# Reordering one step of a windowed-attention and mixture-of-experts kernel: key products ahead of the norm transposes, and norms one row earlier

## The chip, the cores and the metric

The kernel runs on one core of one Trainium2 chip. The metric is the device time of one execution in microseconds (us); lower is better.

## The reference, cut to what matters

The input `x` is 2 images of 128 channels and 256 by 256 pixels, in fp32. Two blocks follow each other, each with its own residual.

```python
x = x + conv(ln_over_channels(x))          # windowed attention
t = tokens(x)                              # one token per pixel, 128 wide
t = t + ffn(ln_over_channels(t))           # 8 experts, the best 2 of them
```

In the attention, `qkv` is a 1x1 product with a 384x128 weight. Queries are 8x8 pixel windows, keys and values are the 12x12 windows around them, in 4 heads of 32. Relative position logits and a fixed mask are added before the softmax. The mask keeps only keys whose row and column distance to the query are of one parity, so the picture falls apart into four independent planes (even or odd rows, even or odd columns). `W_out` is a last 128x128 product. In the feed-forward block a router gives 8 logits per token; the two highest are kept as gates; each token is the gated sum of two experts' 128x128 products.

## The kernel before, in words

A strip is 8 image rows; there are 64 strips (32 for each image). Each strip has four planes, and the main loop makes one step for each plane: `n` counts planes, `i, pl = divmod(n, 4)` gives the strip and the plane in it. In step `n` three things run interleaved:

- **Attention of plane n.** `scores` makes the logits: 16 small products with `au` (L357) and 64 of 64x32 with keys and queries (L372), which run on quarters of the array, then one exponential on ScalarE into `pT`. `attend` makes the sums (`ones`, L391) and 64 small products with the values (L399), then on VectorE `sT`, `rc`, `rT` and the scaled result `o`. `out_project` is the product `po` (L424), which VectorE adds to `xt`.
- **Projections of plane n+1** (`project`, a generator). Before the change its first part makes `pq` (queries) and `pu` (for the position logits), which VectorE brings into `au` by two transposes and two copies (L290 to L300); its second part has POOL gather `xcol` (L305) and makes the two `pk` products (keys, L312), copied by ScalarE to `kcol`; its third part makes `pvv` (values, L329) from `xcol`.
- **Norms, router and experts of finished rows.** `norms` transposes two rows of the strip before (`px_f`) and two rows of a strip ahead (`px_c`) on TensorE (L211), takes their variance on VectorE (`bn_stats`, L213), and gets the reciprocal root through ScalarE. `ln1_c` spreads the result over partitions by four transposes `pb` (L262) and multiplies into `xn` (L265), the normalised input of `project`. `route` turns the logits (`plt`, L444, and `plg`, L466) into `gate` and `gx` in a chain of small VectorE operations (L470 to L496). `experts`, also a generator, runs one step later than its `route`: `pg` transposes the gate (L505) and ScalarE copies it, `pbias` (L511) starts the sum, then four parts of two 128x512 products `pe` each (L520), of which VectorE adds four experts (L531) and ScalarE scales the other four (L535) and POOL adds those (L536 to L540). Another step later `py` (L544) transposes the sum back.

TensorE executes its instructions in program order. The order inside a step is written by hand as a sequence of calls, with `next(...)` between them pulling the generators on; the framework's scheduler keeps that order per engine nearly everywhere and inserts semaphore waits. `parts` is the newest `experts` generator, `behind` the one before it (its `py`), `ahead` is `project`.

All products outside the attention scores share four PSUM buffers (`mm_tile`, `bufs=4`), handed out in turn, so a product can wait for a reader of an earlier one. `xn`, `xcol`, `kcol` and `auT` each have two buffers. A strip's `xn` needs the last two of its rows copied to the next strip's `xn` by POOL (`halo`, L246).

On TensorE the order of a steady step is: pg, L357, L372, px_f, px_c, plt, pbias, pe (t=0), py, ones L391, L399, pe (t=1), plg, pb, pe (t=2), po, pq, pu, pe (t=3), pk, pk, pvv.

Of the kernel before, what the change touches and what calls it, by code (L numbers as in the profile page):

```python
# [10 lines left out]
F32 = mybir.dt.float32  # L11
# [5 lines left out]
P = 128  # L17
# [21 lines left out]
NU = 9  # L39
# [3 lines left out]
def kernel(  # L43
# [16 lines left out]
    nc = tc.nc  # L60
    B, C, H, W = x.shape
    NS = H // R
    PR, PC = R // 2, W // 2
    NP = PC // 8
# [10 lines left out]
    work = ctx.enter_context(tc.tile_pool(name="work", bufs=2))  # L75
# [4 lines left out]
    def mm_tile(name):  # L80
        return ps_mm.tile([P, 512], F32, tag="mm", name=name)
# [8 lines left out]
    strips = [(b, s) for b in range(B) for s in range(NS)]  # L90
# [89 lines left out]
    wrel = ctile([P, P], "wrel")  # L180
# [4 lines left out]
    auT = []  # L185
# [48 lines left out]
    def ln_rows(i):  # L234

        s = strips[i][1]
        return range(1 if s == 0 else 2, KR - 1 if s == NS - 1 else KR)

    def halo(i):

        s = strips[i][1]
        cur = xn[i % 2]
        if s == 0:
            nc.gpsimd.memset(cur[:, :, :, 0, :], 0.0)
        else:
# [12 lines left out]
    def ln1_c(i, k, rs):  # L258

        pb = mm_tile(f"pb{i}_{k}")  # L260
        for t in range(NT):
            nc.tensor.transpose(  # L262
                pb[:, t * P : (t + 1) * P], rs[:, t : t + 1].broadcast_to([P, P]), ident
            )
        nc.vector.tensor_tensor(  # L265
            xn[i % 2][:, :, :, k, 1 : PC + 1],
            ln1_src(i, k).rearrange("p (y j x) -> p y x j", y=2, x=2),
            pb.rearrange("p (y j x) -> p y x j", y=2, x=2),
            ALU.mult,
        )  # L270

    def project(n, state):

        i, pl = divmod(n, 4)
        xp = xn[i % 2][:, pl // 2, pl % 2]
        inner = xp[:, 1 : 1 + PR, 1 : PC + 1]

        pq = mm_tile(f"pq{n}")
        nc.tensor.matmul(pq, lhsT=wq, rhs=inner, start=True, stop=True)  # L279
        qs = work.tile([P, 2 * NP, PR, 4], F32, tag="qs", name=f"qs{n}")  # L280
        nc.scalar.copy(
            qs.rearrange("p m a s -> p a m s"), pq.rearrange("p (a m s) -> p a m s", a=PR, s=4)
        )

        pu = mm_tile(f"pu{n}")
        nc.tensor.matmul(pu, lhsT=wrel, rhs=inner, start=True, stop=True)  # L288
        uT = work.tile([P, PR, 4, 32], F32, tag="uT", name=f"uT{n}")
        nc.vector.transpose(uT, pu.rearrange("p (a m s) -> p a s m", a=PR, s=4))  # L290
        for j in range(2):
            shifted = uT[:, :, :, NU * j + 3 : NU * j + 9]
            dims = [list(d) for d in shifted.ap]
            dims[1 + j][0] -= 1
            nc.vector.tensor_copy(
                auT[n % 2][:, :, :, 6 * j : 6 * j + 6],
                bass.AP(shifted.tensor, shifted.offset, dims),
            )
        au = work.tile([P, 2 * NP, PR, 4], F32, tag="au", name=f"au{n}")
        nc.vector.transpose(au.rearrange("p m a s -> p a s m"), auT[n % 2])  # L300
        yield

        xl, kk = xcol[n % 2], kcol[n % 2]
        for half in range(2):
            nc.gpsimd.tensor_copy(  # L305
                xl[:, :, half, 0:NK].rearrange("p t (r c) -> p t r c", c=KC),
                windows(xp, half * HP, HP),
            )
        for r in range(0, KR, 3):
            pk = mm_tile(f"pk{n}_{r}")  # L310
            nk = 3 * (PC + 2)
            nc.tensor.matmul(  # L312
                pk[:, :nk],
                lhsT=wk,
                rhs=xp[:, r : r + 3, :].rearrange("p r c -> p (r c)"),
                start=True,
                stop=True,
            )
            nc.scalar.copy(
                kk[:, :, r * KC : (r + 3) * KC].rearrange("p t (r c) -> p t r c", c=KC),  # L320
                windows(pk[:, :nk].rearrange("p (r c) -> p r c", r=3), 0, NP),
            )
        yield

        vv = work.tile([P, HP, P], F32, tag="vv", name=f"vv{n}")
        for t0 in range(0, HP, 4):
            pv = mm_tile(f"pvv{n}_{t0}")
            for t in range(4):
                nc.tensor.matmul(  # L329
                    pv[:, t * P : (t + 1) * P],  # L330
                    lhsT=xl[:, t0 + t].rearrange("p a k -> p (a k)"),
                    rhs=wv,
                    start=True,
                    stop=True,
                )
            nc.scalar.copy(vv[:, t0 : t0 + 4, :].rearrange("p t c -> p (t c)"), pv)  # L336
        state.update(qs=qs, kk=kk, au=au, vv=vv)
        yield
# [82 lines left out]
    def out_project(n, state):  # L421
        i, pl = divmod(n, 4)
        po = mm_tile(f"po{n}")
        nc.tensor.matmul(  # L424
            po, lhsT=wo, rhs=state["o"].rearrange("p f z -> p (f z)"), start=True, stop=True
        )
        xv = xt[i].rearrange("p (a y) (m s x) -> p y x m a s", y=2, x=2, s=4)[:, pl // 2, pl % 2]
        nc.vector.tensor_add(xv, po.rearrange("p (m a s) -> p m a s", a=PR, s=4), xv)

    def norms(f, c, nm):  # L430


        st = small.tile([P, 2 * NT, 6], F32, tag="st", name=f"st{nm}", bufs=4)
        n0, n1 = (0 if f else NT), (2 * NT if c else NT)
        lT = None
        if f:
            src = rows_of(*f)
            stats(src, st, f"f{nm}")
        if c:
            stats(ln1_src(*c), st[:, NT:, :], f"c{nm}")  # L440
        if f:
            plt = mm_tile(f"plt{nm}")
            for t in range(NT):
                nc.tensor.matmul(  # L444
                    plt[32 * t : 32 * t + 32, :P],
                    lhsT=rw,
                    rhs=src[:, t * P : (t + 1) * P],
                    start=True,
                    stop=True,
                )  # L450
            lT = work.tile([P, P], F32, tag="lT", name=f"lT{nm}")
            nc.scalar.copy(lT, plt[:, :P])  # L452
        if not (f or c):
            return None, None, None
        r = rstd(st[:, n0:], epsc[:, n0:n1], n1 - n0, nm)
        return (r[:, 0:NT] if f else None), (r[:, NT - n0 :] if c else None), lT
# [96 lines left out]

    halo(0)
    for k in ln_rows(0):
        ln1_c(0, k, norms(None, (0, k), f"_{k}")[1])
    n_planes = 4 * len(strips)
    states = {0: {}}  # L560
    for _ in project(0, states[0]):
        pass
# [1 line left out]
    parts, behind = none, none  # L564
    for n in range(n_planes + 6):
        i, pl = divmod(n, 4)
        live = n < n_planes
        if pl == 0:
            load_x(i + 3)
            if i + 1 < len(strips):  # L570
                halo(i + 1)
        next(parts, None)
        if live:
            scores(n, states[n])
        f = (i - 1, pl) if 0 < i <= len(strips) else None
        rows = list(ln_rows(i + 1))[-4:] if i + 1 < len(strips) else []
        ks = [k for k in rows if (k - 2) % 4 == pl or (k == 1 and pl == 0)]
        if i + 1 < len(strips) and strips[i + 1][1] == 0:
            ks = list(ln_rows(i + 1))[pl::4]
        rf, rc, lT = norms(f, (i + 1, ks[0]) if ks else None, f"_{n}")  # L580
        next(parts, None)
        next(parts, None)
        next(behind, None)
        if live:
            attend(n, states[n])
        next(parts, None)
        routed = (*f, *route(*f, rf, lT)) if f else None
        if ks:
            ln1_c(i + 1, ks[0], rc)
            for k in ks[1:]:  # L590
                ln1_c(i + 1, k, norms(None, (i + 1, k), f"_{n}_{k}")[1])
        next(parts, None)
        if live:
            out_project(n, states.pop(n))
        ahead = none
        if n + 1 < n_planes:
            states[n + 1] = {}
            ahead = project(n + 1, states[n + 1])
        next(ahead, None)
        next(parts, None)  # L600
        next(ahead, None)
        next(ahead, None)
        behind = parts
        parts = experts(*routed) if routed else none


def shape_constants():
# [55 lines left out]
```

## Time and profile before

| | |
|---|---|
| median of 3 runs | 5855.48 us (5855.04 to 5867.62) |
| profiled execution | 5851.49 us; its span 5849.7 us, 1.8 us lie around it |
| TensorE (PE) busy, matmuls | 5470.1 us, 94% of the span |
| VectorE (DVE) / ScalarE (ACT) / POOL busy | 4262.2 / 2504.6 / 2057.8 us |
| mean granted TensorE clock | 0.974 |
| instruction fetch, TensorE's queue (q8) | 755 packets, 12.37 MB |

How to read it: matmul busy time is no measure of distance from the limit, because matmuls overlap; where a step's length is wanted, the start of one L357 group is compared with the start of the next. Times of a step are given below from the start of its L357 group. DVE instructions overlap by about 0.1 us, so a chain is summed from start to start. "issue" is time in which an engine waited for nothing that the profile shows.

### The profile page before, as it was taken

How to read it: one execution, taken by the hardware profiler on the slowest of the kernel's cores; microseconds unless marked ns; L12 is line 12 of the kernel's file. 1: busy time of each engine (PE TensorE's matmuls, PEld its weight loads, DVE VectorE, ACT ScalarE, POOL GpSimd, SP SyncE). 2: the span in 40 equal slices, each digit the busy share in tenths (PEclk: the TensorE clock that was granted, in tenths of full speed). 3: DMA queues.
4: the chain of work that ended last, by engine and by line, in shares of the span. 5: the costliest groups of instructions: out<-in, count | busy, mean ns of one | idle time of the engine just before them, and what ended most of it. 6: DMA issues, size and time to landing. Idle time of an engine off the chain costs nothing.

```text
span 5849.7 us, 221084 instructions
## 1 busy us (share of the span) xinstructions
PE 5470.1 (94%) x95758; PEld 3226.5 (55%) x95758; DVE 4262.2 (73%) x14184; ACT 2504.6 (43%) x7189; POOL 2057.8 (35%) x3667
## 2 busy tenths in 40 slices
PE   6999999999999999999999999999999999999998
PEld 4555555555555555555555555555555555555554
DVE  4767777767767777767767777767767767767766
ACT  2434444444444444444444444444444434434444
POOL 1333333333333333333333333333333333333334
PEclk8999999999999999999999999999999999999998
DMA  1000000000000000000000000000000000000000
GB/s 51 17 31 17 31 24 23 31 17 31 31 17 31 31 17 31 31 17 31 17 31 31 17 31 28 20 31 17 31 31 17 31 24 24 31 17 31 17 9 23
DMA packets 21957, 149.32 MB, mean 26 GB/s; under 512 B 2906, under 2 KB 4602, under 8 KB 4602
## 3 DMA queue, kind: packets, MB, share of 16 engines
q1 hardware_dynamic: 18432, 134.23, 6.1%
q8 instruction: 755, 12.37, 0.9%
q14 instruction: 216, 1.77, 0.1%
q10 hardware_dynamic: 2554, 0.95, 0.1%
HBM read 68.06 MB, written 67.11 MB: 23 GB/s over the span
## 4 chain that ended last, share of the span: by engine, by line
PE 83%; DVE 8%; ACT 6%; issue 2%; DMA 0%; ACTq 0%; POOL 0%; POOLq 0%; DVEq 0%
PE pe L520 32%; PE pvv L329 7%; PE att L372 6%; ACT others L535 6%; PE att L399 5%; PE pbias L511 5%; PE pk L312 4%; PE pq L279 3%; PE pu L288 3%; PE po L424 3%; PE att L357 3%; PE px_f L211 3%; PE att L391 3%; PE py L544 2%; PE px_c L211 2%
## 5 line engine op out<-in xcount | busy, mean ns | idle before, releaser
L520 PE MATMUL pe<-ew,xt 128*128 128x512 f32 x4096 | 2071.4, 629 | 184.0 <-ACT others L535 184.0
L535 ACT ACTIVATE others<-pe,gx 128x128 f32<-128x128 f32 x4096 | 1199.5, 369 | 1874.0 <-PE pe L520 1869.3
L536 POOL TENSOR_TENSOR others<-others 128x256 f32<-128x256 f32 x1024 | 758.3, 741 | 3324.8 <-ACT others L535 3226.3
L531 DVE SCALAR_TENSOR_TENSOR acc<-pe,gx,acc 128x128 f32<-128x128 f32 x4096 | 1394.6, 340 | 339.6 <-PE pe L520 301.3
L520 PEld LDWEIGHTS pe<-ew,xt 128*128 128x128 f32 x4096 | 725.8, 193 | 1123.1 <-issue 542.0
L213 DVE BATCH_NORM_STATS2 st<-px_f 128x6 f32<-128x128 f32 x1024 | 228.3, 286 | 959.8 <-PE px_f L211 959.8
L539 POOL TENSOR_TENSOR acc<-acc,others 128x128 f32<-128x128 f32 x1024 | 479.0, 468 | 262.8 <-DVE acc L531 207.1
L329 PEld LDWEIGHTS pvv<-wt,xcol 128*128 128x128 f32 x4096 | 476.9, 191 | 154.3 <-ACT others L535 114.6
L329 PE MATMUL pvv<-wt,xcol 128*128 128x128 f32 x4096 | 522.8, 281 | 1.7
L540 POOL TENSOR_TENSOR acc<-acc,others 128x128 f32<-128x128 f32 x1024 | 468.1, 457 | 75.6
L372 PE MATMUL att<-qs,kcol 32*64 32x32 f32 x32768 | 404.7, 225 | 68.5 <-issue 68.2
L380 ACT ACTIVATE pT<-att 128x1024 f32<-128x1024 f32 x256 | 262.3, 1025 | 445.1 <-PE att L372 445.1
L372 PEld LDWEIGHTS att<-qs,kcol 32*64 32x64 f32 x32768 | 396.0, 130 | 74.1 <-issue 73.5
L312 PE MATMUL pk<-xn,wt 128*128 128x390 f32 x1024 | 378.0, 491 | 0.0
L399 PEld LDWEIGHTS att<-pT,vv 64*32 64x32 f32 x32768 | 351.6, 105 | 47.5 <-issue 9.9
L336 ACT COPY vv<-pvv 128x512 f32<-128x512 f32 x512 | 300.8, 587 | 165.5 <-PE pvv L329 165.5
L399 PE MATMUL att<-pT,vv 64*32 64x32 f32 x32768 | 348.8, 201 | 5.5 <-issue 5.0
L305 POOL COPY xcol<-xn 128x480 f32<-128x480 f32 x512 | 302.1, 613 | 120.5 <-DVE xn L265 76.4
L511 PE MATMUL pbias<-eb,gT 32*128 32x512 f32 x512 | 311.7, 690 | 2.8 <-ACT lT L452 2.1
L312 PEld LDWEIGHTS pk<-xn,wt 128*128 128x128 f32 x1024 | 195.6, 191 | 194.9 <-issue 91.6
L424 PE MATMUL po<-o,wt 128*128 128x512 f32 x512 | 264.9, 599 | 12.8 <-DVE o L418 12.8
L300 DVE STREAM_TRANSPOSE au<-auT 128x512 f32<-128x512 f32 x256 | 270.5, 1057 | 0.2
(3777 smaller groups left out, 7019.7 us busy)
## 6 DMA issues: line engine op xcount, KB each, us to landing
xt<-in_x_dram SPq DMA_DIRECT2D x64, 1024.0 KB, 4.8
out_dram<-xt SPq DMA_DIRECT2D x64, 1024.0 KB, 5.2
ew<-in_L_ffn_expert_w_dram ACTq DMA_DIRECT2D x1, 512.0 KB
wall<-in_L_conv_W_qkv_dram ACTq DMA_DIRECT2D x1, 192.0 KB
keys<-in_c_keys_dram ACTq DMA_DIRECT2D x1, 64.0 KB, 7.5
wall<-in_L_conv_W_out_dram ACTq DMA_DIRECT2D x1, 64.0 KB
eb<-in_L_ffn_expert_b_dram ACTq DMA_DIRECT2D x4, 4.0 KB
ties<-in_c_ties_dram ACTq DMA_DIRECT2D x1, 32.0 KB
```

Source lines behind the costliest of these rows:

```text
L312: nc.tensor.matmul(pk[:, :nk], lhsT=wk, rhs=xp[:, r : r + 3, :].rearrange("p r c -> p (r c)"), start=True, stop=True,)
L329: nc.tensor.matmul(pv[:, t * P : (t + 1) * P], lhsT=xl[:, t0 + t].rearrange("p a k -> p (a k)"), rhs=wv, start=True, stop=True,)
L372: nc.tensor.matmul(sc[rows, h, 32 * t : 32 * t + 32], lhsT=kk[hp, half * HP + t, :], rhs=qs[hp, m0 : m0 + 2].rearrange("p m a s -> p (m a ...
L399: nc.tensor.matmul(av[hp, half, 32 * t : 32 * t + 32], lhsT=vv[rows, t, hp], rhs=pT[rows, h, 32 * t : 32 * t + 32], start=True, stop=True,)
L424: nc.tensor.matmul(po, lhsT=wo, rhs=state["o"].rearrange("p f z -> p (f z)"), start=True, stop=True)
L511: nc.tensor.matmul(pb, lhsT=gT, rhs=eb.rearrange("r t c -> r (t c)"), start=True, stop=True)
L520: nc.tensor.matmul(pe, lhsT=src[:, t * P : (t + 1) * P], rhs=ew[:, e0 : e0 + 4, :].rearrange("p e c -> p (e c)"), start=True, stop=True,)
L531: nc.vector.scalar_tensor_tensor(acc[:, t, :], pe_e, g, acc[:, t, :], ALU.mult, ALU.add)
L535: nc.scalar.activation(others[:, e - 4, :], pe_e, AF.Copy, scale=g)
L536: nc.gpsimd.tensor_tensor(others[:, 0:2, :], others[:, 0:2, :], others[:, 2:4, :], ALU.add)
L539: nc.gpsimd.tensor_tensor(acc[:, t, :], acc[:, t, :], others[:, 0, :], ALU.add)
L540: nc.gpsimd.tensor_tensor(acc[:, t, :], acc[:, t, :], others[:, 1, :], ALU.add)
```

## The change

Four things change. The first is in `project`: its first part now makes only `pq`; POOL's gather into `xcol` and the two `pk` products become its second half, still ahead of the first `yield`; `pu` with its VectorE work becomes the second part. The second is in the loop: `next(ahead)` comes directly behind `scores`, so `pq`, `pk`, `pk` stand between L372 and the transposes `px_f`, `px_c`; `pu` stands behind pe (t=1), and `py` moves from ahead of `attend` to behind it. The third: since `project(n+1)` now runs early in step n, its rows must be ready one step sooner. `rows_at(n)` names the rows to normalise in step n as those that step n+1 named before; the first of them and `halo(1)` are done in the prologue; `halo(i+2)` moves to the step with `pl == 3`. The fourth: `pg` (the first `next(parts)`) is called at the end of a step instead of at the start of the next.

```diff
     # project(n, state): pu and its VectorE work move behind pk
+        xl, kk = xcol[n % 2], kcol[n % 2]
+        for half in range(2):
+            nc.gpsimd.tensor_copy(...xl..., windows(xp, half * HP, HP))
+        for r in range(0, KR, 3):
+            pk = mm_tile(f"pk{n}_{r}")
+            ...
+        yield
         pu = mm_tile(f"pu{n}")
         ...
         nc.vector.transpose(au.rearrange("p m a s -> p a s m"), auT[n % 2])
-        yield
-        xl, kk = xcol[n % 2], kcol[n % 2]
-        ...
         yield
         vv = ...
```

```diff
+    def rows_at(n):
+        i, pl = divmod(n + 1, 4)
+        i += 1
+        if i >= len(strips):
+            return []
+        rows = list(ln_rows(i))
+        if strips[i][1] == 0:
+            return [(i, k) for k in rows[pl::4]]
+        return [(i, k) for k in rows if k - 2 == pl]
+
     halo(0)
     ...
+    if len(strips) > 1:
+        halo(1)
+    for i, k in rows_at(-1):
+        ln1_c(i, k, norms(None, (i, k), f"_a{k}")[1])
     ...
         if pl == 0:
             load_x(i + 3)
-            if i + 1 < len(strips):
-                halo(i + 1)
-        next(parts, None)
         if live:
             scores(n, states[n])
+        ...
+        next(ahead, None)                     # pq, xcol, pk, pk
+        if pl == 3 and i + 2 < len(strips):
+            halo(i + 2)
         f = (i - 1, pl) if 0 < i <= len(strips) else None
-        ...
+        cs = rows_at(n)
+        rf, rc, lT = norms(f, cs[0] if cs else None, f"_{n}")
         next(parts, None)                     # pbias
         next(parts, None)                     # pe t=0
-        next(behind, None)
         if live:
             attend(n, states[n])
+        next(behind, None)                    # py
         next(parts, None)                     # pe t=1
+        next(ahead, None)                     # pu
         routed = (*f, *route(*f, rf, lT)) if f else None
         ...ln1_c of the rows...
         next(parts, None)                     # pe t=2
         if live:
             out_project(n, states.pop(n))
-        ...
-        next(ahead, None)                     # pq, pu
         next(parts, None)                     # pe t=3
-        next(ahead, None)                     # pk
         next(ahead, None)                     # pvv
         behind = parts
         parts = experts(*routed) if routed else none
+        next(parts, None)                     # pg
```

In the built program the steady order on TensorE becomes: L357 (its first 4 products), pg, L357 (the other 12), L372, pq, pk, pk, px_f, px_c, plt, pbias, pe (t=0), ones, L399, py, pe (t=1), pu, plg, pb, pe (t=2), po, pe (t=3), pvv. VectorE keeps the order of the old step with three differences: `sT` goes ahead of the `py` addition, the `pu` work (L290 to L300 in the old numbering) goes ahead of L471, and the `po` addition goes ahead of L478. POOL does the `xcol` gather of a plane behind L536 of pe (t=3), more than a step ahead of the `pvv` that reads it, except once in a strip, in the step with `pl == 2`: there two gathers and the halo copy stand between its additions for pe (t=1) and pe (t=2), and wait for that step's `xn`.

More of the change, by code (lines that the diff above doesn't have):

```diff
@@ L283, in project @@
         )
[L287 to L300, printed above, removed]
-        yield
         xl, kk = xcol[n % 2], kcol[n % 2]
@@ L322, in project @@
             )
+        yield
+        pu = mm_tile(f"pu{n}")
+        nc.tensor.matmul(pu, lhsT=wrel, rhs=inner, start=True, stop=True)
+        uT = work.tile([P, PR, 4, 32], F32, tag="uT", name=f"uT{n}")
+        nc.vector.transpose(uT, pu.rearrange("p (a m s) -> p a s m", a=PR, s=4))
+        for j in range(2):
+            shifted = uT[:, :, :, NU * j + 3 : NU * j + 9]
+            dims = [list(d) for d in shifted.ap]
+            dims[1 + j][0] -= 1
+            nc.vector.tensor_copy(
+                auT[n % 2][:, :, :, 6 * j : 6 * j + 6],
+                bass.AP(shifted.tensor, shifted.offset, dims),
+            )
+        au = work.tile([P, 2 * NP, PR, 4], F32, tag="au", name=f"au{n}")
+        nc.vector.transpose(au.rearrange("p m a s -> p a s m"), auT[n % 2])
         yield
@@ L552, in store @@
         nc.sync.dma_start(out[b, :, s * R : (s + 1) * R, :], xt.pop(i))
+    n_planes = 4 * len(strips)
+    def rows_at(n):
[7 more added lines that the diff above has]
+        return [(i, k) for k in rows if k - 2 == pl]
     halo(0)
@@ L558 @@
         ln1_c(0, k, norms(None, (0, k), f"_{k}")[1])
-    n_planes = 4 * len(strips)
+    if len(strips) > 1:
+        halo(1)
+    for i, k in rows_at(-1):
+        ln1_c(i, k, norms(None, (i, k), f"_a{k}")[1])
     states = {0: {}}
@@ L569 @@
             load_x(i + 3)
-            if i + 1 < len(strips):
-                halo(i + 1)
-        next(parts, None)
         if live:
             scores(n, states[n])
[L575 to L582, printed above, removed]
-        next(behind, None)
[L584 to L594, printed above, removed]
         ahead = none
@@ L599 @@
         next(ahead, None)
+        if pl == 3 and i + 2 < len(strips):
+            halo(i + 2)
+        f = (i - 1, pl) if 0 < i <= len(strips) else None
+        cs = rows_at(n)
+        rf, rc, lT = norms(f, cs[0] if cs else None, f"_{n}")
+        next(parts, None)
+        next(parts, None)
+        if live:
+            attend(n, states[n])
+        next(behind, None)
         next(parts, None)
         next(ahead, None)
+        routed = (*f, *route(*f, rf, lT)) if f else None
+        if cs:
+            ln1_c(*cs[0], rc)
+            for c in cs[1:]:
+                ln1_c(*c, norms(None, c, f"_{n}_{c[1]}")[1])
+        next(parts, None)
+        if live:
+            out_project(n, states.pop(n))
+        next(parts, None)
         next(ahead, None)
@@ L604 @@
         parts = experts(*routed) if routed else none
+        next(parts, None)
 def shape_constants():
```

## The prediction

> **What bounds the kernel now.** I read the engines' busy time first, then who TensorE waits for, then one steady step in order of time, then a disturbed step.
>
> ```profile
> PE 5470.1 (94%) x95758; PEld 3226.5 (55%) x95758; DVE 4262.2 (73%) x14184; ACT 2504.6 (43%) x7189; POOL 2057.8 (35%) x3667
> ...
> q8 instruction: 755, 12.37, 0.9%
> ```
>
> TensorE sets the end, but VectorE is at 73%. Over 256 steps TensorE fetches 755 blocks of instructions, 2.95 a step. Where a block ends therefore drifts through the step and comes round every 1/(3-2.95) = 20 steps.
>
> ```profile
> PE pe L520 <- ACT others L535: 184.0, 250, 0.8
> PE att L372 <- issue: 68.2, 58, 2.0
> ```
>
> The first is a wait in every step (0.75 us), the second one in some steps. The steady step, 948.8 to 970.2 us:
>
> ```profile
> 950.76 0.66 PE L211 MATMUL px_f<-ident,xt 128*128 128x128 f32 x4
> 951.46 0.89 DVE L213 BATCH_NORM_STATS2 st<-px_f 128x6 f32<-128x128 f32 x4 [3.59 <-PE px_f L211]
> 957.38 0.72 DVE L409 STREAM_TRANSPOSE sT<-att 128x512 f32<-128x512 f32 x1
> 960.55 1.98 PE L520 MATMUL pe<-ew,xt 128*128 128x512 f32 x4 [0.75 <-ACT others L535]
> 960.57 0.73 POOL L536 TENSOR_TENSOR others<-others 128x256 f32<-128x256 f32 x1 [2.27 <-ACT others L535]
> 960.79 0.55 DVE L471 TENSOR_TENSOR lg<-lg,rb 128x32 f32<-128x32 f32 x1
> 967.22 0.19 DVE L494 TENSOR_TENSOR gate<-gate,sm 128x32 f32<-128x32 f32 x1
> 968.60 0.67 DVE L531 SCALAR_TENSOR_TENSOR acc<-pe,gx,acc 128x128 f32<-128x128 f32 x2
> 970.01 0.27 PE L505 MATMUL pg<-ident,gate 128*32 128x128 f32 x1
> ```
>
> TensorE has one hole. VectorE works from 951.46 to 969.27, then idles 3.6 us until the next px_f. `pg` needs VectorE's last addition, with 0.75 us to spare. L471 (0.18 us when alone) ends with the POOL operation it meets: VectorE's operations on two SBUF inputs wait for POOL. This step takes 21.39 us; each fourth one, with the halo copy on POOL, takes 22.05. Their mean is 21.56.
>
> ```profile
> 1168.29 0.42 PE L372 MATMUL att<-qs,kcol 32*64 32x32 f32 x20 [1.19 <-issue]
> 1170.51 2.07 PE L511 MATMUL pbias<-eb,gT 32*128 32x512 f32 x2
> ...
> 1143.00:1165.30 22.30, 20.82 (x377) 12.43 (x376) 16.26 (x55) 9.73 (x29) 6.65 (x13) 1.00 0.01 2
> 1165.30:1192.00 26.70, 24.44 (x379) 13.45 (x379) 17.15 (x55) 10.29 (x29) 9.34 (x17) 0.87 0.01 2
> ```
>
> Near a block's end the small products L357 and L372 (160 in 1.9 us) outrun the fetch. The hole of 1.19 us is followed by a granted clock of 0.87 in that step, and `pbias` takes 2.07 us instead of 1.12. Eight such steps follow each other (21.7, 22.3, 26.7, 26.4, 26.4, 23.3, 22.8, 22.2 us from 1121 us on). Above 21.39 they lose 19.3 us once the 1.3 us of two halo steps are off: 7.8 us of issue holes (0.15, 0.73, 1.19, 1.58, 1.57, 1.59, 0.61, 0.41), 11.5 us of half clock. This comes some 13 times: about 100 us of holes. For the clock, 0.974 of 5849.7 us is 306 us at half speed; 55 lie in the first 150 us and 37 in the tail, so 215 us of the loop, worth 107 us. All 31 drops in steady steps came after a window of 3.4 us with 0.85 to 1.95 us of such idling and at most 0.6 us of pe.
>
> **The change part by part.** *TensorE's own time.* The same instructions run. The pieces of the steady step sum to 20.64 us without the 0.75 us wait. That wait is for ScalarE's four L535 of pe (t=1), free 3.25 us after this pe begins. Now `pb` waits for them, behind pe, pu and plg: 1.79 + 0.86 + 0.11 = 2.76 us, so 0.48 us remain and TensorE alone would need 21.12 us.
>
> *The VectorE loop.* `px_f` moves behind pq, pk, pk: 0.86 + 1.46 = 2.3 us later against L357, while VectorE's work in a step stays. The 0.75 us of spare and the 0.27 us that TensorE gains cannot hold that. I sum the loop from gate to gate, start to start:
> - gate to L213: wake 0.05, pg 0.22, rest of L357 0.37, L372 1.45, pq 0.86, pk 1.46, px_f 0.50, wake 0.20: 5.11 us.
> - L213 to sT, paced by TensorE: px_c 0.53, plt 0.35, pbias 1.05, pe 1.82, ones 0.46, L399 1.30, wake 0.08, less 0.20: 5.39 us.
> - sT to gate, VectorE without a pause: sT 0.75, py addition 0.60, rc 0.25, rT 0.62, o 0.60, the pu work 0.63 + 0.24 + 0.91, xn 0.60, po addition 0.60, twelve L531 3.10, the router's eleven operations 1.86: 10.76 us.
>
> The sum is 21.26 us. Collisions with POOL come on top. POOL's L536 for pe (t=2) becomes ready within 0.05 us of L478's start, and L536 for pe (t=3) lies on L494. If L478 goes first and only L484 and L494 wait, 0.2 to 0.5 us; if POOL goes first, L478 takes 1.28 us instead of 0.43, as it does in the halo steps of before, and the sum is 0.75. So 21.5 to 22.0 us; I take 21.8, since VectorE seems first by a hair. In the step with pl == 2 POOL does two gathers (0.56 each) and the halo (1.06) where L474, L478 and L484 stand, and the additions behind them move onto L490 and L494: 1.1 to 1.4 us above 21.26, 22.5 us. The mean is (3 x 21.8 + 22.5)/4 = 21.98, against 21.56: +0.42 us in 250 steps, **+105 us** (bounds: -10 to +150, from 21.35 and 22.2 and 22.0 and 22.6). What waits behind `pg` is TensorE itself, with 12 of L357's products; behind the halo on POOL, the additions of the experts, which nobody needs before `py`.
>
> *The clock.* Holes at the end of L372 stay, since L357, L372 and the count of instructions stay. The holes that fell in px_f and plt (0.61 and 0.41 us) now meet pq and pk, 2.3 us of work in 6 products: 13 x 1.0 = **-13 us**. The window that trips the clock can now hold only L357, L372, the wait at pg and the hole, as full products stand on both sides; before, the transposes, plt and pbias belonged to it (drops came when the window ended 2.95 to 6.4 us after L357 began; now 3.3 to 5.2 at most). That is some six tenths of the drops, and full products behind them should end them after one window of 3.4 us instead of the 6.7 us of now. 215 us becomes 70 to 130, worth 45 us less at least and 75 at most: **-60 us**. Bounds: nothing, if the wait at pg adds as much idling as the products save, to -107 us.
>
> The rule that speaks against this: the Trainium skill, page "TensorE: Matmul & The Clock Gate", table "Why this matters for your kernels", asks only that no idle gap exceeds about 3 us. By it holes of 1.2 us would cost no clock and the change would win none; the sum would be 60 us higher. The rows above show the drop at 1.19 us.
>
> *Prologue.* One row's norm and `xn`, not hidden: VectorE 0.8 + 1.5 + 0.7, with transposes and ScalarE some 4 us; a step at the end loses it, hidden. **+4 us.** `py`, `pg` and `halo` keep their counts; the loads and stores on SP keep their steps.
>
> Sum: 5851.5 + 105 - 13 - 60 + 4 = 5887.5. The runs' median lies 4 us above the profiled execution: **5892 us**.
>
> **The rivals.**
> - *VectorE keeps up* (ends faster). Its mechanism: L478 and L484 slip between POOL's operations, the steady step takes 21.35 to 21.45 us and the pl == 2 step 22.1. For it: the loop without collisions is 21.26, and only 0.05 us decides L478. Against it: L494 meets L536 in any case. It decides below a mean step of 21.84, where +0.28 x 250 = 70 us no longer exceeds what the clock gives back. Mean 21.6: +10 - 13 - 60 to -100 + 4, so 5753 to 5793 on this execution, about 5785 with runs.
> - *The clock gains nothing.* The wait at pg is idling inside the same small stretch, and TensorE drops as often. 5851.5 + 105 - 13 + 4 = 5948, with runs 5950.
> - *All drops vanish*, the VectorE loop as forecast: 5851.5 + 105 - 13 - 107 + 4 = 5841, with runs 5845, at the edge of faster.
>
> **How the numbers follow.** Forecast 0.42, VectorE keeps up 0.32, no gain of clock 0.16, all drops gone 0.10. A measurement of this kernel tells 0.2%, 12 us, from no change. Faster takes 0.32 and 0.05; same takes 0.05 of the last and 0.02 of the forecast's low end; slower takes 0.40 and 0.16. The forecast's own range, by its bounds, is 5855 to 5930; the range that takes in the other cases is 5755 to 5970.
>
> **What would show it.** Right: the wait "pe L520 <- ACT others" gone, a wait of `pb` on it near 0.5 us; a wait of `pg` on the gate (L494) of 0.3 to 0.9 us in nearly every step, longer in each fourth; VectorE's idle time before L213 shorter than 3.6 us; steps of 21.8 and 22.5 us; holes of issue still in L372, hardly any in px_f; a mean clock of 0.980 to 0.988. Wrong: no wait of `pg`, steps at or below 21.4 us (the loop was over-counted), a clock as before or at 0.99, or a new wait that I have not named.

## The result and the profile after

The changed kernel takes 5948.91 us (median of 4 runs, 5928.62 to 5954.03), the kernel before, on the same chip, 5861.55 us (5855.04 to 5870.24, 4 runs): ratio 1.0142, 95% interval 1.0112 to 1.0171. It is slower by 1.4%, and slower was forecast; the forecast was 5892 us, 57 us too low. The profiled execution took 5946.92 us, its span is 5945.1 us.

The page of the changed kernel, busy time of the engines and TensorE's instruction fetch:

```profile
PE 5557.1 (93%) x95758; PEld 3269.4 (55%) x95758; DVE 4037.3 (68%) x14192; ACT 2552.1 (43%) x7191; POOL 2023.6 (34%) x3667
...
q8 instruction: 754, 12.35, 0.9%
```

TensorE executes the same number of matmuls, 95758, and VectorE is busy 225 us less, mostly because its operations meet POOL's elsewhere (in the steps shown L471 took 0.55 us before and takes 0.17 now). None of that shortens the kernel. Who TensorE waits for (total us, times, longest us):

```profile
PE pg L505 <- DVE gate L494: 120.3, 255, 2.7
PE att L372 <- issue: 98.3, 63, 2.1
PE pb L262 <- ACT others L535: 81.4, 244, 0.4
```

The first line is the new wait: `pg` waits for VectorE's gate in every step. The second, idle time in L372 that no other engine ends, was 68.2 us; such idle time is called a hole below. The third takes the place of the 184.0 us for which pe (t=1)'s buffer was waited for before, and is less than half of it. One regular step, 955.89 to 977.82 us, in order of time:

```profile
961.07 0.60 PE L211 MATMUL px_f<-ident,xt 128*128 128x128 f32 x4
961.71 0.89 DVE L213 BATCH_NORM_STATS2 st<-px_f 128x6 f32<-128x128 f32 x4 [4.56 <-PE px_f L211]
964.71 0.35 DVE L531 SCALAR_TENSOR_TENSOR acc<-pe,gx,acc 128x128 f32<-128x128 f32 x1 [0.82 <-PE pe L520]
967.20 0.72 DVE L409 STREAM_TRANSPOSE sT<-att 128x512 f32<-128x512 f32 x1 [0.70 <-PE att L399]
974.82 0.72 POOL L536 TENSOR_TENSOR others<-others 128x256 f32<-128x256 f32 x1 [2.13 <-ACT others L535]
974.86 0.96 DVE L478 TENSOR_TENSOR cmp<-lg 128x256 f32<-128x256 f32 x1
978.34 0.21 DVE L494 TENSOR_TENSOR gate<-gate,sm 128x32 f32<-128x32 f32 x1
978.69 0.27 PE L505 MATMUL pg<-ident,gate 128*32 128x128 f32 x1 [0.42 <-DVE gate L494]
```

L357 begins at 977.82, and `pg` can only begin at 978.69, 0.1 us behind the gate. VectorE works from 967.20 to 978.77 without a pause worth naming; in each step it waits 4.56 us for `px_f`, then twice more on its way to `sT`. A regular step takes 21.92 us (21.39 before), each fourth one, now the one with `pl == 2`, 22.29 (22.05). And a disturbed step:

```profile
1111.66 1.15 PE L372 MATMUL att<-qs,kcol 32*64 32x32 f32 x89
1114.89 0.68 PE L372 MATMUL att<-qs,kcol 32*64 32x32 f32 x31 [2.08 <-issue]
1115.50 2.08 PE L279 MATMUL pq<-xn,wt 128*128 128x512 f32 x2
1117.37 2.81 PE L294 MATMUL pk<-xn,wt 128*128 128x390 f32 x4
```

```profile
1110.10:1137.20 27.10, 24.26 (x379) 14.16 (x378) 15.67 (x56) 9.94 (x28) 7.57 (x15) 0.87 0.01 2
```

The hole in L372 is 2.08 us (the longest in all of before was 2.0), the mean granted clock of the step is 0.87, and `pq` and `pk`, the full products put behind L372, take about twice as long as in a regular step: 2.08 us instead of 1.13 and 2.81 instead of 1.47. The trace's records of the granted clock hold 1 and 0.5 alone; a stretch at 0.5 is called a drop below, and the time in drops half clock.

The time between the two profiles, 95 us, comes from the 246 steps between the starts of step 6 and step 252 (5526.5 us before, 5619.3 after; "steps 6 to 252" below); the first L357 comes 4.4 us later, the steps 0 to 5 take 14.6 us less, and what follows the start of step 252 takes 12.8 us more.

### The profile page after: what moved, and what is told of

The parts are those of the page before. It is cut to its first block, busy times and chain, and to the rows that moved or that the text cites. A ratio compares the mean times of both kernels' runs of the same rounds, so it can differ in the third digit from the quotient of the medians.

```text
span 5945.1 us, 220905 instructions
## 1 busy us (share of the span) xinstructions
PE 5557.1 (93%) x95758; PEld 3269.4 (55%) x95758; DVE 4037.3 (68%) x14192; ACT 2552.1 (43%) x7191; POOL 2023.6 (34%) x3667
## 4 chain that ended last, share of the span: by engine, by line
PE 66%; DVE 26%; ACT 4%; issue 4%; DMA 0%; ACTq 0%; POOL 0%; POOLq 0%
PE pe L520 20%; DVE acc L531 9%; PE pk L294 6%; PE att L372 6%; PE pq L279 5%; PE att L399 5%; PE pbias L511 5%; DVE cmp L478 4%; ACT others L535 4%; PE po L424 3%; DVE xt L428 3%; PE att L391 2%; PE att L357 2%; PE pb L262 2%; PE px_f L211 2%
## 5 line engine op out<-in xcount | busy, mean ns | idle before, releaser
L520 PE MATMUL pe<-ew,xt 128*128 128x512 f32 x4096 | 1990.6, 609 | 4.9 <-ACT others L535 2.3
L536 POOL TENSOR_TENSOR others<-others 128x256 f32<-128x256 f32 x1024 | 754.6, 737 | 3311.3 <-ACT others L535 3304.9
L531 DVE SCALAR_TENSOR_TENSOR acc<-pe,gx,acc 128x128 f32<-128x128 f32 x4096 | 1402.3, 342 | 244.4 <-PE pe L520 234.5
L520 PEld LDWEIGHTS pe<-ew,xt 128*128 128x128 f32 x4096 | 703.2, 190 | 891.3 <-issue 266.9
L213 DVE BATCH_NORM_STATS2 st<-px_f 128x6 f32<-128x128 f32 x1024 | 228.2, 286 | 1372.5 <-PE px_f L211 1372.5
L329 PEld LDWEIGHTS pvv<-wt,xcol 128*128 128x128 f32 x4096 | 516.0, 191 | 168.6 <-issue 122.2
L329 PE MATMUL pvv<-wt,xcol 128*128 128x128 f32 x4096 | 546.6, 281 | 16.5 <-DVE acc L531 16.5
L372 PE MATMUL att<-qs,kcol 32*64 32x32 f32 x32768 | 430.8, 225 | 98.3 <-issue 98.3
L372 PEld LDWEIGHTS att<-qs,kcol 32*64 32x64 f32 x32768 | 421.8, 131 | 105.5 <-issue 105.5
L294 PE MATMUL pk<-xn,wt 128*128 128x390 f32 x1024 | 418.2, 533 | 2.5 <-issue 2.4
L399 PEld LDWEIGHTS att<-pT,vv 64*32 64x32 f32 x32768 | 347.9, 105 | 39.7 <-issue 2.9
L399 PE MATMUL att<-pT,vv 64*32 64x32 f32 x32768 | 343.0, 200 | 2.6 <-issue 2.6
L279 PE MATMUL pq<-xn,wt 128*128 128x512 f32 x512 | 322.2, 713 | 3.3 <-issue 1.8
L301 ACT COPY kcol<-pk 128x480 f32<-128x480 f32 x512 | 288.2, 563 | 83.5 <-PE pk L294 47.8
L409 DVE STREAM_TRANSPOSE sT<-att 128x512 f32<-128x512 f32 x256 | 183.5, 717 | 178.9 <-PE att L399 178.8
```

Of the source, the lines that this page charges most:

```text
L294: nc.tensor.matmul(pk[:, :nk], lhsT=wk, rhs=xp[:, r : r + 3, :].rearrange("p r c -> p (r c)"), start=True, stop=True,)
L329: nc.tensor.matmul(pv[:, t * P : (t + 1) * P], lhsT=xl[:, t0 + t].rearrange("p a k -> p (a k)"), rhs=wv, start=True, stop=True,)
L372: nc.tensor.matmul(sc[rows, h, 32 * t : 32 * t + 32], lhsT=kk[hp, half * HP + t, :], rhs=qs[hp, m0 : m0 + 2].rearrange("p m a s -> p (m a ...
L399: nc.tensor.matmul(av[hp, half, 32 * t : 32 * t + 32], lhsT=vv[rows, t, hp], rhs=pT[rows, h, 32 * t : 32 * t + 32], start=True, stop=True,)
L520: nc.tensor.matmul(pe, lhsT=src[:, t * P : (t + 1) * P], rhs=ew[:, e0 : e0 + 4, :].rearrange("p e c -> p (e c)"), start=True, stop=True,)
L531: nc.vector.scalar_tensor_tensor(acc[:, t, :], pe_e, g, acc[:, t, :], ALU.mult, ALU.add)
```

## The experiments

The theory after the result has two parts. **Loop:** what stands on TensorE between `pg` and the last products that VectorE needs for the next gate, and what VectorE does between them, makes the step; `pq` and `pk` got into that loop. **Block:** instructions reach TensorE in blocks, and where a step begins in its block decides whether L372 runs dry; holes make the drops of the clock. The 755 packets of 12.37 MB are 16.4 KB each; the trace of before has 193,333 instructions for TensorE, semaphore waits included (four for an fp32 product, two for a transpose), so an instruction is 64 bytes and a packet 256 of them. By this count a step is 754.9 instructions before and 754.1 after. In the kernel before, the mean hole is at most 0.03 us for steps that begin at instruction 0 to 90 or 208 to 255 of a block, and 1.0 to 1.6 us from 117 to 155; after, there is none outside 117 to 194 but in two steps (0.8 us each, in `pe`), and it is 1.3 to 1.6 us from 130 on. That was the reason for the experiments with added transposes.

All times are medians; the kernel before took 5847.21 us beside e1 to e4 (7 runs), 5847.19 beside e5 to e8 (9 runs), 5850.54 beside e9 and e10 (8 runs). Steps, holes ("issue") and half clock are of the steps 6 to 252 of the profiled execution. Regular and fourth step are those without hole or drop, but in e10, where every step has a hole. The profiled execution of e2, 5978.56 us, is the fastest of its four.

| | us | ratio (95%) | regular, fourth step | holes us | us at half clock |
|---|---|---|---|---|---|
| before | see above | 1 | 21.39, 22.05 | 90 | 215 |
| after | 5948.91 | 1.0142 (1.0112 to 1.0171) | 21.92, 22.29 | 100 | 184 |
| e1 pg behind pk | 5636.39 | 0.9632 (0.9606 to 0.9657) | 21.07, 21.44 | 66 | 61 |
| e2 norms first | 6023.32 | 1.0302 (1.0271 to 1.0333) | 22.07, 22.44 | 114 | 167 |
| e3 products mixed | 5762.56 | 0.9848 (0.9826 to 0.9869) | 21.95, 22.31 | 1 | 7 |
| e4 before, padded | 5714.83 | 0.9768 (0.9747 to 0.979) | 21.70, 22.36 | 0 | 7 |
| e5 products later | 6054.88 | 1.035 (1.032 to 1.038) | 21.73, 22.14 | 119 | 492 |
| e6 e1, padded | 5520.57 | 0.9444 (0.942 to 0.9467) | 21.07, 21.44 | 3 | 7 |
| e7 after, padded | 5726.17 | 0.9794 (0.977 to 0.9819) | 21.92, 22.28 | 3 | 3 |
| e8 one split | 5608.96 | 0.9594 (0.9569 to 0.9619) | 21.34, 21.70 | 1 | 7 |
| e9 pu late | 5899.12 | 1.0076 (1.0051 to 1.0102) | 21.60, 22.64 | 96 | 137 |
| e10 e4, moved in the block | 6823.01 (one run) | | about 27 | 404 | 1389 |

**e1: pg moved behind pq, pk, pk.**

```diff
         next(ahead, None)          # pq, pk, pk
+        next(parts, None)          # pg
         ...
         parts = experts(*routed) if routed else none
-        next(parts, None)          # pg
```

> The changed kernel with one call moved: pg is issued behind pq, pk, pk instead of at the end of the step, so TensorE meets the gate some 4 us later. Theory A (the loop gate, pg, px_f, VectorE, gate sets the changed step's length): the wait of pg on L494 goes, the steady step falls from 21.92 to 21.1 to 21.3 us (TensorE's own 20.64 and a wait of pb of 0.3 to 0.5), and the time to 5740 to 5790 us. Theory B (TensorE's own new order is longer; its modelled busy time in a step is 21.17 us against 20.64 before, and the pb wait comes on top): the wait only moves, the step stays at 21.5 us or more, 5830 us or more. On the issue holes of L372: if the wait at pg had taken the instruction stream's lead away, they fall from a maximum of 2.1 us back to 1.6 us.

The wait at `pg` is gone and the step is 21.07 us: TensorE's own 20.64, the wait of `pb`, 0.33, and 0.1 more; the waits of this kernel are led by

```profile
PE pb L262 <- ACT others L535: 81.0, 244, 0.4
PE att L372 <- issue: 64.9, 63, 2.1
PE pg L505 <- DVE gate L494: 13.0, 5, 2.6
```

The third line is 5 steps at the start, as in the kernel before. The loop theory's step came out. The whole is faster than the 5740 to 5790 us expected because holes and half clock fell too: 66 and 61 us, against 100 and 184 with the wait, with the same products behind L372. That speaks for the wait as what feeds them, though e1 also takes `pg` out from among the products of L357. The kernel before, where `pg` stands ahead of L357, speaks for the wait too: there every fourth step, the one behind the halo step, waits 0.29 us at `pg`, and for steps that begin at instruction 143 to 181 of a block the mean hole is 1.62 us with this wait (10 steps) and 1.04 without it (29 steps). At instruction 130 to 144 the wait makes no difference (1.57 and 1.66 us in before, 1.67 and 1.64 in e10).

**e2: the norms ahead of pq, pk.** The lines of `f`, `cs` and `norms` go between `scores` and the first `next(ahead)`; `pg` stays.

```diff
         if live:
             scores(n, states[n])
+        f = ...; cs = rows_at(n)
+        rf, rc, lT = norms(f, cs[0] if cs else None, f"_{n}")
         ...
         next(ahead, None)          # pq, pk, pk
-        f = ...; cs = rows_at(n)
-        rf, rc, lT = norms(f, cs[0] if cs else None, f"_{n}")
```

> The changed kernel with px_f, px_c and plt ahead of pq, pk, pk again, as in the kernel before; pg, py and pu stay where the change put them. Theory A: VectorE starts its step 2.3 us earlier, the gate is ready before pg, no wait at pg; steady step 21.1 to 21.3 us, 5740 to 5810 us. Theory B (the other moves cost it): step 21.5 us or more, 5830 us or more. On the clock: with the transposes next to L372 again, drops as long as before (some 6.7 us each) if the full products behind L372 are what ends them in the changed kernel; 4.6 us each otherwise.

A miss: the wait at `pg` stays at 0.42 us and the step is 22.07. So it is not the place of `px_f` that lengthened the loop, though the prediction had it so. From gate to L213 VectorE now takes 2.87 us instead of 5.09, but from there to `sT` 7.86 instead of 5.49: with its statistics done early it waits longer for pe (t=0) (L531) and L399, since `pq` and `pk` now stand ahead of those. On the clock: the drops are 4.4 us each, as short as in the changed kernel, though the transposes stand next to L372 again; full products directly behind L372 are not needed for that.

**e3: the products mixed into the small ones.** e1 with `pq` between L357 and L372 and a `pk` after three and after six of L372's eight parts.

```diff
+        next(between, None)                    # pq, behind L357
         for t in range(HP):
+            if t in (3, 6):
+                next(between, None)            # pk
             ...                                # 8 products of L372
```

> e1 with pq put between L357 and L372, the first pk behind 24 of the 64 L372 products of 32 columns (48 of its 128 instructions), the second behind 48. Theory F (holes come where 256 instructions of small products are used up faster than the next block of instructions arrives, and the clock drops where holes make a window idle): any 256 instructions now hold a full product of 0.7 to 0.9 us, so holes shrink from about 95 us in all to under 30, drops of the clock from 40 to under 10, and the time is 100 to 180 us below e1, about 5600 to 5660. Theory G (the holes are a matter of bandwidth or of the number of small products, wherever they stand): within 30 us of e1.

The holes and the drops go, but the step rises by 0.88 us to 21.95. One step of e3:

```profile
1362.72 1.13 PE L279 MATMUL pq<-xn,wt 128*128 128x512 f32 x2
1363.77 0.73 PE L376 MATMUL att<-qs,kcol 32*64 32x32 f32 x48
1364.43 0.92 PE L295 MATMUL pk<-xn,wt 128*128 128x390 f32 x2
```

From start to start `pq` takes 1.05 us here and 0.96 in e1, three eighths of L372 0.66 instead of 0.55. Six changes between small and full products more, 0.15 us each. Cured and paid for: 5762.56, not the 5600 to 5660 expected.

**e4: the kernel before, with a step of 768 instructions.** No change of order: seven transposes of 32x32 more in each step, into unread columns of `plt`, and seven once in the prologue; 768 is three blocks, so every step begins at instruction 29 to 34 of its block.

```diff
+            for _ in range(7):
+                nc.tensor.transpose(plt[:32, P : P + 32], ident[:32, :32], ident[:32, :32])
```

> The kernel before with 7 transposes of 32x32 into an unread part of plt's buffer in each step, which brings TensorE's instructions of a step from 755 to 768, three blocks of 256, and 7 more ahead of the loop, which set each step's start to 30 instructions into a block. In the kernel before, steps that start 0 to 90 or 195 to 255 instructions into a block have no issue hole, those from 90 to 195 have 0.2 to 1.6 us. Theory F: no holes and no drops of the clock in the whole loop, for about 0.2 us of transposes per step: 5855 - 224 + 50, so 5650 to 5710 us. Theory G (the run of eight disturbed steps in twenty has another cause than where a block ends): 5855 to 5910 us.

No hole in steps 6 to 252, one drop, and 5 us more than the range expected. The kernel before is 132 us faster although it does more work (0.31 us a step), with no change of order.

**e5: the products behind L399.** The changed kernel with the first `next(ahead)` moved behind `attend`.

```diff
-        next(ahead, None)          # behind scores
         ...
             attend(n, states[n])
+        next(ahead, None)          # pq, pk, pk
         next(behind, None)         # py
```

> The changed kernel with pq, pk, pk taken from behind scores to behind attend (L399); pg stays at the end of a step, before the next L357. Theory (the 2.3 us of pq and pk between pg and sT lengthen VectorE's loop from gate to gate): the loop becomes 21.26 - 2.3 + collisions = 19.0 to 19.7 us, below TensorE's own 21.1, so the wait at pg is gone, a regular step is 21.1 to 21.2 us and the fourth 21.4 to 21.6. The disturbed steps stay (about 200 us, as the stretch from L357 to plt is again without a full product): 5700 to 5780 us. Rival (it is pg's place at the end of the step that costs): a wait of about 0.4 us stays in every step and a step is 21.8 us or more: 5880 to 5960 us.

A miss. The wait at `pg` stays, and the step is 21.73 us. VectorE's `sT` comes 2.2 us earlier (9.14 us into the step instead of 11.30), but from there to the gate it takes 13.31 us instead of 11.35, since it now waits for `py` and pe (t=1), which stand behind `pq` and `pk`:

```profile
978.50 0.69 DVE L545 TENSOR_TENSOR xt<-py,xt 128x512 f32<-128x512 f32 x1 [0.32 <-PE py L544]
979.36 0.35 DVE L531 SCALAR_TENSOR_TENSOR acc<-pe,gx,acc 128x128 f32<-128x128 f32 x1 [0.17 <-PE pe L520]
```

Before this run I had put the loop's length down to what lies between `pg` and `sT`; e2 and e5 together say that it is everything up to the gate. The whole is slower than both expectations, because the wait stands again in one stretch with L357, L372, the transposes and `plt`: 492 us at half clock, the most of all but e10, in drops of 7.7 us each.

**e6: e1 with added transposes.** 6 or 7 transposes of 32x32 a step behind `plg`, where `pb` waits anyway; 13 instructions more on the mean. (The expectation speaks of 761 instructions; by the trace e1's step has 755.1 and this one 768.1, three blocks, and 768 packets were fetched.)

```diff
         nc.tensor.transpose(plg[:, :P], lT, ident)
+        for _ in range(6 + k % 2):
+            nc.tensor.transpose(plg[:32, P : P + 32], ident[:32, :32], ident[:32, :32])
```

> The kernel of e1 (pg behind pq, pk, pk) with 6 or 7 transposes of 32x32 more per step, on unread columns of plg, just ahead of pb, where TensorE waits 0.33 us anyway. They make a step 761 (on the mean 760.75) instructions of TensorE, 2.97 blocks of 256, so that every step from the 5th to the last begins between instruction 24 and 83 of its block, a place at which no step of before or of e1 was disturbed. Theory (the place in the block makes the holes, the holes make the drops): hardly any hole in L372, fewer than 5 drops, the loop 246 x 21.16 = 5205 us + 0 to 20 us, and the whole 5500 to 5560 us. If the added transposes are not hidden, 0.3 us a step more: 5580 to 5630. Rival (holes come of something else, such as the density of small products since some earlier step): holes and drops as in e1, 5630 to 5700 us.

```profile
911.48 0.27 PE L466 MATMUL plg<-ident,lT 128*128 128x128 f32 x1
911.68 0.37 PE L468 MATMUL plg<-ident 32*32 32x32 f32 x7
912.07 0.65 PE L262 MATMUL pb<-ident,r__41_14349 128*128 128x128 f32 x4
```

The seven small transposes fill the wait, `pb` shows none behind them, and the step stays at 21.07 us. One drop is left in the steps 6 to 252. This is the fastest version of the study: 5520.57 us, 5.6% below the kernel before and by the two ratios 6.9% below the changed one.

**e7: the changed kernel with the same transposes.** Seven each step, at the same place; steps begin at instruction 26 to 87.

> The changed kernel with 7 transposes of 32x32 more per step just ahead of pb; steps begin at instruction 27 to 87 of their block, where none was disturbed. This takes the disturbed steps out of the change and leaves the loop of VectorE. Theory: steps of 21.9 and 22.3 us as before (the wait at pg takes up what the transposes cost), a wait at pg of 0.4 us in every step, hardly a hole or drop: 246 x 22.02 = 5417 us + 0 to 20, and 60 + 170 around it: 5645 to 5700 us. Rival (the wait at pg by itself drops the clock or makes holes): over 10 drops, 5750 us or more.

The steps are those of the changed kernel, the wait at `pg` is there in all (255 times), one drop is left: 5422 us for 246 steps against 5417 expected. (The total expected left out the first six steps, some 90 us.) So the wait alone makes no drop: it needs the hole. And it parts the change's account: without most holes and drops the changed kernel takes 223 us less (5948.91 - 5726.17), 197 us of it in the steps 6 to 252 (5619.3 - 5422.2).

**e8: one split.** e1 with `pq`, `pk`, `pk` together in the middle of L372 (`if t == 4`).

> The kernel of e1 with pq, pk, pk put together into the middle of L372 (after 32 of its 64 products) instead of behind it. Theory: the full products let the fetch catch up, so holes fall from 66 us to under 20 us and drops from 17 to under 6; the price is one change from small to full products and back more, 0.25 to 0.35 us a step (e3 had three such places at 0.88 us together). Step 21.3 to 21.45 us: 246 x 21.5 = 5290 us + 20 to 50 + 222: 5530 to 5580 us. Rival (what e3 lost was pq and pk in L357's and L372's way as such, not the changes): 0.6 us or more a step, 5640 us and more.

Holes 1 us, one drop, 0.27 us more a step: two changes more at 0.13 us each. As expected in the step; the total (326 us around the loop, where 222 were put) is 29 us above the range.

**e9: pu back ahead of pe (t=3).** The loop shortened on VectorE's side, with all else of the change left as written.

```diff
         next(parts, None)          # pe t=1
-        next(ahead, None)          # pu
         ...
             out_project(n, states.pop(n))
+        next(ahead, None)          # pu
         next(parts, None)          # pe t=3
```

> The changed kernel with pu taken from behind pe (t=1) back to its old place ahead of pe (t=3); pq, pk, pk, pg and all else stay as the change put them. VectorE then takes L322 (0.91 us) and three L531 (0.26 us each) behind the gate instead of ahead of it. Theory (what stands between two gates, on TensorE or on VectorE, makes the step): the loop of 21.93 us loses 1.7 us and is 20.2 us, below TensorE's own 20.64 + 0.75 us (the wait of pe (t=2) for L535 comes back with pu's going): no wait at pg, a regular step 21.4 us, the fourth about 22, mean 21.5. With pg free the holes and drops shrink to about those of e1 (some 120 us): 246 x 21.5 = 5289 + 120 + 325 around the loop: 5700 to 5790 us. Rival (pg's place at the end of the step, or pq and pk behind L372, cost by themselves): a wait at pg of 0.4 us stays and a step is 21.8 us or more, 5880 us and more.

In three steps of four `pg` waits no more (65 times in place of 255). The built program's order is not the one written, though: in 241 of the 246 steps `pq` stands ahead of L357, and `pg` ahead of it:

```profile
964.33 0.27 PE L505 MATMUL pg<-ident,gate 128*32 128x128 f32 x1
964.49 1.13 PE L279 MATMUL pq<-xn,wt 128*128 128x512 f32 x2
965.84 0.70 PE L357 MATMUL att<-au,keys 32*64 32x128 f32 x32 [0.22 <-DVE au L322]
```

`pq` and `pk` still stand between `pg` and `px_f`, so the lost wait speaks for the loop, which VectorE's work left; on `pg`'s place among the products of L357 this run says nothing. L357 now waits for L322, the last of `pu`'s work, and in each fourth step POOL's copies still hold the gate up, by 0.99 us; the mean step is 21.86 us, not 21.5:

```profile
PE pe L520 <- ACT others L535: 185.6, 250, 0.8
PE att L372 <- issue: 96.7, 86, 2.2
PE pg L505 <- DVE gate L494: 72.7, 65, 2.6
PE att L357 <- DVE au L322: 55.7, 243, 0.3
```

Half a miss, then: 5899.12 us where 5700 to 5790 were expected. Holes stay at 96 us with a wait of 0.22 us at the start of the step; e1, with no wait there, has 66.

**e10: e4, moved in the block.** e4 with 62 transposes in the prologue instead of 7; the steps are the same instruction for instruction and all but one begin at instruction 140 to 144.

> The kernel of e4 (before, with 7 small transposes more per step, so that a step is 768 instructions, 3 blocks of 256) with 55 more transposes of 32x32 once, in the prologue: every step begins at about instruction 140 of its block instead of 30. The steps themselves are instruction for instruction those of e4. Theory (the place in the block makes the hole): every step has a hole of about 1.5 us in L372 and most a drop of the clock, 25 to 27 us a step: 6500 to 7000 us, where e4 took 5715. Rival (the added transposes cured e4 in another way, or the block is not what counts): as e4, 5715 to 5730 us.

```profile
1064.65 1.48 PE L376 MATMUL att<-qs,kcol 32*64 32x32 f32 x122
1067.91 0.31 PE L376 MATMUL att<-qs,kcol 32*64 32x32 f32 x6 [1.78 <-issue]
...
1070.07 2.07 PE L517 MATMUL pbias<-eb,gT 32*128 32x512 f32 x2
```

245 steps of 246 have such a hole in L376 (L372 of the other kernels), and in the step shown `pbias` takes 2.07 us behind it instead of 1.12; 178 drops make 1389 us at half clock. 55 tiny transposes, once, cost 1108 us. That settles where a step begins as the cause: same steps, another place. That it is the fetch of the next block which comes too late fits the count of instructions and packets; no record shows the fetch and the hole side by side.

## Why the prediction was right or wrong

| term | forecast | measured | from |
|---|---|---|---|
| undisturbed steps | +105 us | +113 | mean 22.01 against 21.555, 246 steps; e7: 22.04 nearly without holes |
| holes | -13 | +11 | 89.7 to 100.4 us |
| clock | -60 | -15 | half of 215 less 184 us |
| prologue | +4 | +4.4 | first L357 at 60.5 instead of 56.1 |

These four make 113 us; the profiles differ by 95. The steps 0 to 5 and the tail take 2 us off. What the other steps lose over their undisturbed length fell by 20 us (224 to 204), of which holes and clock explain 4; the other 16 are not explained.

The direction was right: slower, and by the loop. The size was put too small: 5948.91 us lies inside the 5755 to 5970 us that take in the rivals, but above the 5855 to 5930 us that the prediction called its own range by its bounds. Its bounds add up to more than that, some 5730 to 5997 us; and the lower bound of the loop, from steps of 21.35 and 22.2 us, is 0 and not -10.

**TensorE's own time: right.** 21.12 us forecast; e1, where the wait at `pg` is gone, has 21.07. Two misses of a tenth of a microsecond cancel in it: the wait of `pb` is 0.33 instead of 0.48, the rest 20.74 instead of 20.64.

**The loop: right in size, and the wait named.** Its three pieces, in the step shown above, are 5.09, 5.49 and 11.35 us, 21.93 in all, where 5.11, 5.39 and 10.76 plus collisions of 0.54 were put. The third is 0.59 longer than its sum without collisions. That the mean step came out at 22.01 where 21.98 was put is partly luck: the regular step is 0.12 us above the forecast, the fourth 0.21 below it. The wait at `pg` is 0.42 us in the regular steps and in the fourth alike; it was to be longer there. What was left open, who is first at L478, POOL won by 0.04 us (974.82 against 974.86), and L478 took 0.96 us instead of 0.43. The Trainium skill, page "SBUF — State Buffer", section "Who interferes with whom", says that a VectorE instruction with two SBUF inputs contends with a GpSimd instruction that reads SBUF. This case agrees: L478, begun 0.04 us behind L536, ends 0.28 us behind its end.

**The reason given for the loop was too narrow.** The prediction tied it to `px_f` coming 2.3 us later. e2 put `px_f` back and the step got longer; e5 put the products behind L399 and the wait stayed. What counts is that 2.3 us of products stand anywhere between `pg` and the last product ahead of the next gate; e1 took them out by moving `pg`, e9 took VectorE's work out instead and lost the wait in three steps of four. The list of signs was wrong by the sum's own figures, too: 5.11 us from gate to L213 leaves VectorE some 4.6 us idle there, and not under 3.6.

**The clock: the term that failed.** 40 drops instead of 32, each shorter (4.6 us instead of 6.7): 184 us, where 70 to 130 were forecast; the granted clock came to 0.977, below the 0.980 to 0.988 named as a sign. That full products soon behind L372 end the drops sooner fits the lengths: 3.6 us in e1, 4.4 in e2, 7.7 in e5. But the term had only six tenths of the drops left, since it took the small stretch to be shorter and the holes in it to stay. The holes over 1.2 us became 60 instead of 35, and a drop began in 39 of them or within 5 us behind (27 before). In e1, with the same products behind L372 and no wait at the step's start, there are 21 such holes, 12 of them with a drop, and half clock is 61 us; in e9, with a wait of 0.22 us there and `pq` ahead of L357, 45, 24 and 137 us. The term came out near its bound "nothing, if the wait at pg adds as much idling as the products save". The rival "the clock gains nothing", 5950 us, lies nearest the measurement and had a chance of 0.16; that it comes within 2 us is luck, since its terms +105, -13 and 0 came out as +113, +11 and -15, with 18 us the other way that it did not hold.

The rule weighed against this, from the Trainium skill, page "TensorE: Matmul & The Clock Gate", table "Why this matters for your kernels", that no idle gap should exceed about 3 us, is not enough in this case: no hole in e10 is over 2.2 us, and of the 4.5 us by which its mean step is longer than that of e4 (26.37 against 21.89), 2.8 us are loss by half clock (1389 / 2 us in 246 steps).

**The holes: wrong sign.** Those at the transposes did go (20.7 us to nearly nothing, with 4 us in `pq` and `pk`), as forecast. Those in L372 grew from 66.9 to 94.5 us, and the forecast had them stay. In e1 they are 63.7. e1, and the steps of before with and without a wait, put the growth with the wait at the step's start; how the wait lengthens a hole, no run shows.

What the change could have won, e1 shows: 211 us. It put four things together, of which one, `pg` at the end of a step with `pq` and `pk` behind it, turned a gain of 3.7% into a loss of 1.4%.

## What to carry to other kernels

Where two engines hand results back and forth, sum the loop from one hand-over to the same one in the next step: full products that are moved count wherever they stand between the two, so move the hand-over past them, not them past a reader. When groups of steps are disturbed with a steady period, count the instructions of a step against those of a fetched block before reordering anything: a few instructions of padding, put where the engine waits anyway, won more here (116 us on top of e1) than they cost. And price each change between small and full products before splitting a group.

## What was not expected of the hardware

- Where a step begins in its block of 256 instructions decides on holes of up to 2.2 us in a run of small products: the same steps take 21.89 us on the mean from instruction 30 and 26.37 us from instruction 140 (e4, e10).
- A hole of 1.2 to 2.1 us among small products can be enough for the clock to halve for 3.4 to 6.8 us (39 of 60 such holes in the changed kernel); a wait of 0.42 us in each step without such a hole is not (e7: one drop).
- A change between small products on parts of the array and full ones costs about 0.13 to 0.15 us on TensorE (e3: 0.88 us for six; e8: 0.27 for two).
